# A two-layer graph attention and a neighbour sum: a tile's own-node product moved from the second to the third pass, and its seen edges added three steps ahead

## The chip, the core and the metric

The kernel runs on one core of a Trainium2 chip. The time is the device time of one execution, in microseconds (us). TensorE is called PE here (PEld its weight loads), VectorE DVE, ScalarE ACT, GpSimd POOL, and SyncE, which issues most transfers, SP.

## The reference, cut to what matters

There are N = 12500 nodes with 256 features and E = 200000 edges (`src`, `dst`, and a weight each).

```python
h = relu(layernorm(x))
e = h @ W_P_w + W_P_b + W_pos                 # 128 wide
for layer in range(2):                        # attention over the edges, 8 heads of 16
    q, k, v = (e[src] @ qT), (e[dst] @ kT), (e[dst] @ vT)
    att = exp(clip(sum_of_head(q * k), -10, 10))
    agg = segment_sum(att * v, src) / (segment_sum(att, src) + 1e-8)
    e = layernorm(agg + e) * ln_s + ln_b
x = x + e @ inv_w + inv_b                     # 256 wide
h = relu(layernorm(x))
agg = segment_sum(edge_weight * (h @ w_nbr)[src], dst)
out = x + agg + h @ w_own + bias
```

## The kernel before

Nodes lie in NT = 98 tiles of 128. A head (0 to about 650 us) sorts the edges, embeds the nodes and makes the plan of the edges, with a test (`bad`) that decides between a general and a short arm; these inputs take the short arm, `short_arm`. In it the order of the instructions on every engine is the order of the program text (a manual schedule); the waits between engines come from the tiles that they share.

**Two attention passes** (`short_attention`, layers 0 and 1). The edges of an attention layer are grouped by the tile of `src`. Edges whose other end is in the first SB = 3 tiles are "seen": SEEN = 3 columns of 128 edges a tile, whose keys and values are taken from `kvn` in SBUF by a one-hot product on PE. The others are "far": 1304 columns, STEP = 8 of them a step, 163 steps. For a far step POOL issues eight gathers (line 802) of k and v rows from DRAM into `kvg` (three buffers, issued two steps ahead); ACT spreads positions into one-hot tiles (L1186, L1190); PE takes the queries (`take_q`, L1205) from `q` by a tile number in a register; DVE makes the logits (L1215) and the weighted values; PE sums them by node into `ps` (`sums`, L1244 and L1246); DVE adds `ps` into `acc` (`adds`, L813).

The loop over the steps calls the far functions in a fixed order and, between them, the work that was put into named slots of that step:

```python
put(slots, (t0 - 5, "load", load), (t0 - 3, "act_seen", spread_hot), (t0 - 2, "pe_seen", take),
    (t0 - 2, "act_k", copy_k), (t0 - 2, "dve_seen", logits), (t0 - 2, "act_last", exps),
    (t0 - 1, "dve_seen_v", weighted), (t0 - 1, "pe_sums", sums), (t0, "dve_adds", add))
```

This is a tile's seen work (`seen`). A tile's far edges are complete at a step called `before` (at least one more than that of the tile ahead of it: 2, 4, 6, 7, 9, 11, 12, 14 ...). Before the change `seen` is given that step as `t0`, and so is what follows a tile's sums, `after`: in layer 0 `next_layer` (normalize, then the next q, k, v: `qkv`), in layer 1 `neighbour_rows`. That runs over some ten steps: normalize; `outwards` (L1012 to L1014: the product with `inv_w`, plus x by an identity product, plus the bias), kept in DRAM as `res_d`; a second normalization; `turn_c` (transpose), `relu` (ACT, into `ht`, L1046); `both` (L1051: products of `ht` with `w_nbr` and `w_own` side by side, 512 wide, and L1053, the bias onto the second half); `rows` (ACT: L1057 copies the first half for a store into the DRAM table `th`, L1059 copies the second half into `acc1`, two tensors of 128 columns that reuse `q` and `acc`); `store`.

**The third pass** (`short_neighbours`) groups the edges by the tile of `dst` in 196 steps of K2 = 8 columns. POOL gathers rows of `th` (L802) into `kvg`, two steps ahead; DVE makes weighted one-hot tiles one step ahead (`edge_hot`, L1343, two buffers); PE multiplies (`sums`, L1356 and L1358: two groups of four columns and one more product each); DVE adds into `acc1` (`adds`, L813). When a tile has all its columns, `result` adds `xt` (its rows of `res_d`, loaded by SP three steps ahead) to `acc1` in two additions (L1378) and stores the rows. Before a step's `sums` PE loads tile numbers of the next step into registers, from `near` (loaded by SP at L1312 for two steps). The order of a step is: transfers, gathers for t + 2, `edge_hot` for t + 1, `adds` of t − 1, results, registers for t + 1, `sums` of t.

Of the kernel before, what the change touches and what calls it, by code (L numbers as in the profile page):

```python
# [27 lines left out]
F32 = mybir.dt.float32  # L28
# [86 lines left out]
def gnn_kernel(ctx, tc, x, src, dst, edge_weight, wp_w, wp_b, w_pos, q1, k1, v1, ln1_s, ln1_b,  # L115
# [19 lines left out]
    part_neg = const.tile([P, SB], F32, name="part_neg")  # L135
    for b in range(SB):
        nc.vector.tensor_scalar(part_neg[:, b:b + 1], part_f, -1.0, float((1 - b) * P), op0=OP.mult, op1=OP.add)
    bad = const.tile([P, 9], F32, name="bad")
    nc.vector.memset(bad, 0.0)
    none = const.tile([1, P], BF16, name="none")  # L140
    nc.vector.memset(none, 0.0)
# [56 lines left out]
    emb_d = [dram.tile([NT * P, D], F32, name=f"emb{i}") for i in range(2)]  # L198
    last_d = dram.tile([NT * P, D], F32, name="last")
    res_d = dram.tile([NT * P, GD], F32, name="res")  # L200
    place_d = dram.tile([P, W], BF16, name="place_d")

    near_d = [dram.tile([1, CG * P // RC, RN], I32, name=f"near{i}") for i in range(2)]
# [13 lines left out]
    def rows_of(t):  # L217
        return min(P, N - t * P)
# [123 lines left out]
    def columns_out(pool, psum, a, b, c):  # L342
# [48 lines left out]
        by_step = lambda t: t[:, 0:FAR].rearrange("p (n k) -> p n k", k=STEP)  # L391
        firsts = t8[:, 0:FAR:STEP]
        fits = c[0:1, STEPS * (STEP + 2):STEPS * (STEP + 3)]
        nc.vector.tensor_tensor(fits, t8[:, STEP::STEP], firsts, op=OP.subtract)
        nc.vector.tensor_scalar(fits, fits, 1.0, None, op0=OP.is_gt)
        nc.vector.tensor_reduce(bad[0:1, 1:2], fits, AX.X, OP.max)
        nc.vector.tensor_scalar(fits, firsts, SLOPE, SLOPE + SLACK - 1.0, op0=OP.mult, op1=OP.add)
        nc.vector.tensor_tensor(fits, fits, step_row, op=OP.is_lt)
        nc.vector.tensor_reduce(fits[:, 0:1], fits, AX.X, OP.max)
        nc.vector.tensor_tensor(bad[0:1, 1:2], bad[0:1, 1:2], fits[:, 0:1], op=OP.add)  # L400
        nc.vector.tensor_scalar(t8, t8, float(NT - 1), None, op0=OP.min)
        nc.vector.tensor_copy(table[:, :, 0:STEP], by_step(t8))
        same = b[0:1, 0:FAR].rearrange("p (n k) -> p n k", k=STEP)
# [594 lines left out]
    def neighbour_rows(node, slots, weights, acc, acc1, t0, t):  # L998

        n = rows_of(t)  # L1000
        inv_sb, w2_sb = weights
        tiles, t1 = attended_later(node, slots, acc, t0, t, 1)
        t2 = even(t1 + 1)
        t3 = next_free(slots, "turn_c", t2 + 2)

        def load():
            xt = tiles["xt"] = node.tile([P, GD], F32, name="xt", bufs=2)
            nc.sync.dma_start(xt[:n], x[t * P:t * P + n, :])

        def outwards():  # L1010
            po = tiles["po"] = slots["psum"].tile([P, 4 * P], F32, name="out_e", tag="n1")
            nc.tensor.matmul(po[:n, 0:GD], tiles["et"][:, :n], inv_sb, start=True, stop=False)  # L1012
            nc.tensor.matmul(po[:n, 0:GD], ident[:n, :n], tiles["xt"][:n], start=False, stop=False)
            nc.tensor.matmul(po[:n, 0:GD], ones_b[:, :n], rows3[:, 0, :], start=False, stop=True)  # L1014

        def copy_all():
            y = tiles["all"] = node.tile([P, GD], F32, name="all", bufs=3)
            nc.scalar.copy(y[:n], tiles["po"][:n, 0:GD])

        def keep_all():  # L1020
            nc.sync.dma_start(res_d[t * P:t * P + n, :], tiles["all"][:n])

        def whole():
            tiles["mv"] = moments(node, tiles["all"][:n], n)

        def root():
            deviation(tiles["mv"], n, eps5)

        def normal():
            mv = tiles["mv"]  # L1030
            nc.vector.reciprocal(mv[:n, 1:2], mv[:n, 1:2])
            off = tiles["off"] = node.tile([P, 1], F32, name="off")
            nc.vector.tensor_scalar(off[:n], mv[:n, 0:1], mv[:n, 1:2], -1.0, op0=OP.mult, op1=OP.mult)

        def centred():
            c = tiles["c"] = node.tile([P, GD], F32, name="c", bufs=2)
            nc.scalar.activation(c[:n], tiles["all"][:n], AF.Identity, bias=tiles["off"][:n], scale=tiles["mv"][:n, 1:2])

        def turn_c():
            pt = tiles["pt2"] = slots["psum"].tile([P, 4, P], F32, name="turn_c", tag="n2")  # L1040
            for k in range(2):
                nc.tensor.transpose(pt[:, k, :n], tiles["c"][:n, k * P:(k + 1) * P], ident[:n, :n])

        def relu():
            ht = tiles["ht"] = node.tile([P, 2, P], F32, name="ht", bufs=1)
            nc.scalar.activation(ht[:, :, :n], tiles["pt2"][:, 0:2, :n], AF.Relu)  # L1046

        def both():
            pz = tiles["pz"] = slots["psum"].tile([P, 4 * P], F32, name="out_c", tag="n2")
            for k in range(2):  # L1050
                nc.tensor.matmul(pz[:n], tiles["ht"][:, k, :n], w2_sb[:, k].rearrange("p a b -> p (a b)"),  # L1051
                                 start=(k == 0), stop=False)
            nc.tensor.matmul(pz[:n, GD:], ones_b[:, :n], rows3[:, 1, :], start=False, stop=True)  # L1053

        def rows():
            h = tiles["h"] = node.tile([P, GD], F32, name="out_rows")
            nc.scalar.copy(h[:n], tiles["pz"][:n, 0:GD])  # L1057
            for h, to in enumerate(acc1):
                nc.scalar.copy(to[:n, t, :], tiles["pz"][:n, GD + h * D:GD + (h + 1) * D])  # L1059

        def store():
            nc.sync.dma_start(th[t * P:t * P + n, :], tiles["h"][:n])

        put(slots, (t1 - 1, "load", load), (t1, "pe_out", outwards), (t1 + 1, "act_out", copy_all),
            (t1 + 1, "store", keep_all), (t1 + 1, "dve_next", whole), (t2, "act_root", root), (t2 + 1, "dve_next", normal),
            (t2 + 1, "act_root", centred), (t3, "pe_turn", turn_c), (t3, "act_turn", relu),
            (t3, "pe_out", both), (t3 + 1, "act_out", rows), (t3 + 1, "store", store))

    def short_attention(wide, pool, psum, still, q, acc, layer, after, early=None):

# [88 lines left out]
                (t0 - 2, "act_k", copy_k), (t0 - 2, "dve_seen", logits), (t0 - 2, "act_last", exps),  # L1159
                (t0 - 1, "dve_seen_v", weighted), (t0 - 1, "pe_sums", sums), (t0, "dve_adds", add))  # L1160

        before = -1
        for t in range(NT):
            before = max(before + 1, (ends_by(t) - 1) // STEP + 1)
            seen(t, before)
            after(slots, before, t)

        def load(i):
# [134 lines left out]
            other_work("store")  # L1303
            t += 1

    def short_neighbours(wide, pool, psum, acc1, plan):
        steps = MAIN // K2
        of = {}

# [58 lines left out]
                f(i)  # L1368

        def load_own(t):  # L1370
            xt = of["xt", t] = pool.tile([P, GD], F32, name="xt", bufs=6)
            nc.sync.dma_start(xt[:rows_of(t)], res_d[t * P:t * P + rows_of(t), :])

        def result(t):
            n, xt = rows_of(t), of.pop(("xt", t))
            for h, to in enumerate(acc1):
                half = slice(h * D, (h + 1) * D)
                nc.vector.tensor_add(xt[:n, half], to[:n, t, :], xt[:n, half])  # L1378
            nc.sync.dma_start(out[t * P:t * P + n, :], xt[:n])


# [4 lines left out]
        for t in range(-4, steps + 1):  # L1386
            if t % 2 == 0:
                do(load, t // 2 + 2, steps // 2)
            for i in outs.get(t + 3 if t + 3 < steps else -1, ()):
                load_own(i)  # L1390
            if t == steps - 1:
                for i in outs[steps]:
                    load_own(i)
            if t == -4:
                for i in range(2):
                    do(gathers, i)
                next_tiles()
            if t >= 0:
                do(gathers, t + 2)
            do(edge_hot, t + 1)  # L1400
            do(adds, t - 1)
            if t < steps:
                for i in outs.get(t, ()):
                    result(i)
            do(registers, t + 1)
            do(sums, t)
        for i in outs[steps]:
            result(i)

    def short_arm(q, acc, acc1):  # L1410
        with tc.tile_pool(name="short", bufs=1) as wide, tc.tile_pool(name="short_p", bufs=1, space=PSUM) as psum, \
# [3 lines left out]
            nc.scalar.copy(still[:, 0:P], iota_f)  # L1415
            with tc.tile_pool(name="short_a", bufs=1) as pool, tc.tile_pool(name="short_n", bufs=2) as node:
                inv_sb = pool.tile([P, GD], F32, name="inv_sb")
                w2_sb = pool.tile([P, 2, 2, GD], F32, name="w2_sb")

                def load_weights():  # L1420
                    layer_rows(pool, True)
                    nc.sync.dma_start(inv_sb, inv_w)
                    for j, w in enumerate((w_nbr, w_own)):
                        nc.sync.dma_start(w2_sb[:, :, j, :], w.rearrange("(k p) n -> p k n", p=P))

                weights = (inv_sb, w2_sb)
                short_attention(wide, pool, psum, still, q, acc, 0,
                                lambda slots, t0, t: next_layer(node, slots, q, acc, t0, t), load_weights)
                short_attention(wide, pool, psum, still, q, acc, 1,
# [1 line left out]
            with tc.tile_pool(name="short_b", bufs=1) as pool:  # L1431
                weights = pool.tile([P, MAIN + MAIN // K], F32, name="plan2")
                nc.scalar.dma_start(weights[:, 0:MAIN], plan_d[2][:, 0:MAIN])
                plan = (idx_a, place_a[:, 0:MAIN + MAIN // K], weights)
                short_neighbours(wide, pool, psum, acc1, plan)


    def results(acc1):
# [66 lines left out]
    with tc.tile_pool(name="sort_a", bufs=1) as sp, tc.tile_pool(name="node_a", bufs=2) as node, \  # L1505
# [30 lines left out]
            embed(node, npsum, wp_sb, zb3, ones_b, q, (t,))  # L1536
        for _ in plan_as_they_come(cp, cpsum):
            pass
        pb = cpsum.tile([P, 9], F32, name="pb", tag="turned")
        nc.tensor.matmul(pb[0:1], ones[:, 0:1], bad, start=True, stop=True)  # L1540
        any_bad = cp.tile([1, 1], F32, name="any_bad")
        nc.vector.tensor_reduce(any_bad, pb[0:1], AX.X, OP.add)
# [37 lines left out]
```

## Time and profile before

| | |
|---|---|
| Median of 11 runs | 7351.35 us (7342.39 to 7369.84) |
| Profiled execution | 7346.42 us, span 7344.6 us |
| Mean granted TensorE clock | 0.802 |
| Busy, share of the span | PE 68%, PEld 56%, DVE 56%, ACT 37%, POOL 54% |
| First pass, first to last far sums | 692 to 2770 us |
| Second pass, first to last far sums | 2830 to 5042 us |
| Third pass, first to last gather | 5080 to 7332 us |

The times of a profile are those of the one profiled execution, on its own clock from the first instruction. In a group's line stand line, engine, operation and tile, the shape, the count, busy time and mean duration; in a list of waits the engine and line that waited, for what, the total, the times and the longest. "issue" is time in which an engine waited for nothing that the profile shows, "remote" a wait whose releaser the profile does not place. Ends of matmuls are modelled.

### The profile page before, as it was taken

How to read it: one execution, taken by the hardware profiler on the slowest of the kernel's cores; microseconds unless marked ns; L12 is line 12 of the kernel's file. 1: busy time of each engine (PE TensorE's matmuls, PEld its weight loads, DVE VectorE, ACT ScalarE, POOL GpSimd, SP SyncE). 2: the span in 40 equal slices, each digit the busy share in tenths (PEclk: the TensorE clock that was granted, in tenths of full speed). 3: DMA queues.
4: the chain of work that ended last, by engine and by line, in shares of the span. 5: the costliest groups of instructions: out<-in, count | busy, mean ns of one | idle time of the engine just before them, and what ended most of it. 6: DMA issues, size and time to landing. Idle time of an engine off the chain costs nothing. (4 is left out here: it accounts for less than half of the span.)

```text
span 7344.6 us, 91646 instructions
## 1 busy us (share of the span) xinstructions
PE 4969.0 (68%) x26262; PEld 4115.0 (56%) x26262; DVE 4096.3 (56%) x9525; ACT 2689.6 (37%) x4814; POOL 3980.4 (54%) x4189
## 2 busy tenths in 40 slices
PE   6773777777777776777777878777555555555555
PEld 3443666666666665666666666664444444444444
DVE  8776666666666665666666666664333333333334
ACT  3442555555555554555555555553000000000000
POOL 0002555555555554555555555554666666666666
PEclk7566888898888887988998888888777777777777
DMA  3112444444444443444444454443333333333333
GB/s 98 56 58 75 126 131 130 130 132 127 128 126 128 131 123 116 128 131 129 127 136 128 125 134 128 128 130 98 93 94 97 99 99 103 105 107 107 110 112 110
DMA packets 536717, 839.01 MB, mean 114 GB/s; under 512 B 105934, under 2 KB 360093, under 8 KB 536235
## 3 DMA queue, kind: packets, MB, share of 16 engines
q0 software_dynamic: 200448, 547.62, 25.7%
q1 hardware_dynamic: 334617, 284.29, 14.0%
q8 instruction: 245, 4.01, 0.2%
q14 instruction: 237, 1.94, 0.1%
q10 hardware_dynamic: 1170, 1.15, 0.1%
HBM read 752.73 MB, written 79.91 MB: 113 GB/s over the span
## 5 line engine op out<-in xcount | busy, mean ns | idle before, releaser
L802 POOL DMA_INDIRECT kvg<-tkv,idx_a x2608 | 2468.5, 947 | 2538.0 <-issue 1309.7
L802 POOL DMA_INDIRECT kvg<-th,idx_a x1568 | 1498.9, 956 | 812.8 <-issue 451.7
L1356 PE MATMUL ps<-kvg,hot 128*128 128x256 f32 x3136 | 1047.6, 482 | 1000.5 <-issue 890.1
L1356 PEld LDWEIGHTS ps<-kvg,hot 128*128 128x128 f32 x3136 | 757.4, 247 | 1225.1 <-issue 1053.2
L1343 DVE TENSOR_SCALAR hot<-iota_f,place_a,plan 128x128 f32<-128x128 f32 x1960 | 521.2, 360 | 1433.3 <-remote 1271.8
L1244 PE MATMUL ps<-kvg,hot 128*128 128x136 f32 x5216 | 838.2, 307 | 358.3 <-issue 339.3
L1215 DVE TENSOR_TENSOR kvg<-qe,kvg 128x512 f32<-128x512 f32 x652 | 431.5, 687 | 1106.4 <-remote 427.1
L1244 PEld LDWEIGHTS ps<-kvg,hot 128*128 128x128 f32 x5216 | 744.7, 210 | 448.1 <-issue 386.9
L1205 PE MATMUL qe<-q,hot_t 128*128 x5216 | 839.0, 312 | 131.0 <-issue 66.0
L1205 PEld LDWEIGHTS qe<-q,hot_t 128*128 128x128 f32 x5216 | 762.5, 224 | 174.4 <-issue 85.1
L1122 PE MATMUL qe<-kvn,hot_s 128*128 128x128 f32 x4720 | 704.2, 301 | 99.2 <-issue 97.6
L1122 PEld LDWEIGHTS qe<-kvn,hot_s 128*128 128x128 f32 x4720 | 659.6, 217 | 111.1 <-issue 110.1
L1186 ACT ACTIVATE far<-spread,part_neg 128x1280 bf16<-128x1280 bf16 x326 | 446.3, 1369 | 20.6 <-issue 9.8
L1190 ACT ACTIVATE hot_t<-far,ones 128x1280 f32<-128x1280 bf16 x326 | 444.9, 1365 | 0.5
L1229 DVE TENSOR_TENSOR hot<-still,place_a 128x1152 f32<-128x1152 f32 x326 | 439.4, 1348 | 0.0
L1153 PE MATMUL qe<-rows_s,hot_e 128*128 128x136 f32 x1176 | 233.7, 348 | 291.4 <-DVE rows_s L1145 214.3
L1234 DVE TENSOR_TENSOR kvg<-still,kvg 128x1024 f32<-128x1024 f32 x326 | 395.0, 1212 | 24.3 <-ACT kvg L1223 16.4
L1217 DVE TENSOR_REDUCE att<-kvg 128x64 f32<-128x1024 f32 x326 | 397.8, 1220 | 11.2
L1153 PEld LDWEIGHTS qe<-rows_s,hot_e 128*128 128x128 f32 x1176 | 194.8, 239 | 331.0 <-issue 239.0
L813 DVE TENSOR_TENSOR acc<-acc,ps 128x256 f32 (+1 forms) x718 | 304.9, 425 | 109.8 <-PE ps L1246 45.5
L1102 ACT ACTIVATE far<-seen,part_neg 128x256 bf16<-128x256 bf16 (+1 forms) x588 | 337.9, 639 | 0.8
L1358 PE MATMUL ps<-kvg,hot 128*128 x784 | 295.1, 463 | 32.8 <-issue 31.9
(253 smaller groups left out, 6492.2 us busy)
## 6 DMA issues: line engine op xcount, KB each, us to landing
spread<-place_d SPq DMA_DIRECT2D x326, 256.0 KB
kvg<-tkv,idx_a POOLq DMA_INDIRECT x2608
kvg<-th,idx_a POOLq DMA_INDIRECT x1568
xt<-in_x_dram SPq DMA_DIRECT2D x194, 128.0 KB
spread<-ext_d SPq DMA_DIRECT2D x326, 64.0 KB
seen<-place_d SPq DMA_DIRECT2D x196, 96.0 KB
seen<-other SPq DMA_DIRECT2D x196, 96.0 KB
emb<-e SPq DMA_DIRECT2D x194, 64.0 KB
```

The costliest lines, as they stand in the source:

```text
L802: nc.gpsimd.indirect_dma_start(out=dest, out_offset=None, in_=table, in_offset=bass.IndirectOffsetOnAxis(ap=idx, axis=0))
L1122: nc.tensor.matmul(to[:, k, :], hot_t[:, at, :], kvn[:, b, half], start=(i == 0), stop=(i == len(have) - 1))
L1153: nc.tensor.matmul(out_of, its["hot"][:, k, :], its["rows"][:, k, :], start=(k == 0), stop=(k == SEEN - 1))
L1186: nc.scalar.activation(far, of.pop(("spread", i)), AF.Abs, bias=part_neg[:, 1:2])
L1190: nc.scalar.activation(hot_t.rearrange("p k e -> p (k e)"), of.pop(("far", i)), AF.Relu, bias=ones[:, 0:1], scale=-1.0)
L1205: nc.tensor.matmul(qe[:, k, :], hot_t[:, h * K + k, :], q[:, bass.ds(tiles[h * K + k], 1), :], start=(k == 0), stop=False)
L1215: nc.vector.tensor_mul(kk, qe, kk)
L1217: nc.vector.tensor_reduce(att, kvg[:, :, 0:D].rearrange("p k (h d) -> p k h d", d=HD), AX.X, OP.add)
L1229: nc.vector.tensor_tensor(hot, iota_p[:, None, :].to_broadcast([P, STEP + 1, P]), place_a[:, c:c + STEP + 1, None].to_broadcast([P, STEP + ...
L1244: nc.tensor.matmul(ps[:, bass.ds(at, 1), :].rearrange("p a b -> p (a b)") if k else ps[:, 0, :], of["hot", i][:, k, :], of["kvg", i][:, k, ...
L1343: nc.vector.tensor_scalar(hot[:, k, :], iota_f, plan[1][:, c:c + 1], plan[2][:, c:c + 1], op0=OP.is_equal, op1=OP.mult)
L1356: nc.tensor.matmul(ps[:, bass.ds(at, 1), :].rearrange("p a b -> p (a b)") if k else ps[:, 0, :], hot[:, w * K + k, :], hg[:, k, :], start= ...
```

## The change

- The second pass makes only the product with `w_nbr` (`both` becomes two 256-wide products, with no bias). `ht` (relu of the normalized rows, transposed) is stored into a new DRAM tensor `ht_d`, 128 KB a tile; `ht` has two buffers in place of one. The two ACT copies into `acc1` go; two memsets on DVE clear the tile's part of `acc1` instead (`nothing`).
- The third pass loads `ht` and `xt` of a tile four steps ahead of its result (`xt` was loaded three ahead), and a new `own` on PE makes `ht` × `w_own` + `xt` (identity product) + bias in PSUM, behind the `sums` of the step ahead of the result. `result` adds that PSUM tile to `acc1`, again in two additions. `w_own` is loaded at the start of the third pass.
- In both attention passes a tile's seen work is put at `at`, at most three steps ahead of `before` (1, 2, 3, 4, 6, 8, 9, 11 ...); the work behind a tile's sums stays at `before`.
- In the test of the plan a partial result is put into a tenth column of `bad` in place of the second, and tile numbers are capped at NT ahead of it.

```diff
@@ neighbour_rows
         def relu():
-            ht = tiles["ht"] = node.tile([P, 2, P], F32, name="ht", bufs=1)
+            ht = tiles["ht"] = node.tile([P, 2, P], F32, name="ht", bufs=2)
             nc.scalar.activation(ht[:, :, :n], tiles["pt2"][:, 0:2, :n], AF.Relu)
         def both():
+            nc.sync.dma_start(ht_d[t][:, :, :n], tiles["ht"][:, :, :n])
             pz = tiles["pz"] = slots["psum"].tile([P, 4 * P], F32, name="out_c", tag="n2")
             for k in range(2):
-                nc.tensor.matmul(pz[:n], tiles["ht"][:, k, :n], w2_sb[:, k].rearrange("p a b -> p (a b)"),
-                                 start=(k == 0), stop=False)
-            nc.tensor.matmul(pz[:n, GD:], ones_b[:, :n], rows3[:, 1, :], start=False, stop=True)
+                nc.tensor.matmul(pz[:n, 0:GD], tiles["ht"][:, k, :n], w_sb[:, k], start=(k == 0), stop=(k == 1))
         def rows():
             h = tiles["h"] = node.tile([P, GD], F32, name="out_rows")
             nc.scalar.copy(h[:n], tiles["pz"][:n, 0:GD])
-            for h, to in enumerate(acc1):
-                nc.scalar.copy(to[:n, t, :], tiles["pz"][:n, GD + h * D:GD + (h + 1) * D])
+        def nothing():
+            for to in acc1:
+                nc.vector.memset(to[:, t, :], 0.0)
...
-            (t3, "pe_out", both), (t3 + 1, "act_out", rows), (t3 + 1, "store", store))
+            (t3, "pe_out", both), (t3 + 1, "act_out", rows), (t3 + 1, "dve_adds", nothing), (t3 + 1, "store", store))
@@ short_attention
-        before = -1
+        before, at = -1, 0
         for t in range(NT):
             before = max(before + 1, (ends_by(t) - 1) // STEP + 1)
-            seen(t, before)
+            at = max(at + 1, before - 3)
+            seen(t, at)
             after(slots, before, t)
@@ short_neighbours
         def load_own(t):
-            xt = of["xt", t] = pool.tile([P, GD], F32, name="xt", bufs=6)
-            nc.sync.dma_start(xt[:rows_of(t)], res_d[t * P:t * P + rows_of(t), :])
+            n = rows_of(t)
+            xt = of["xt", t] = pool.tile([P, GD], F32, name="xt", bufs=8)
+            nc.sync.dma_start(xt[:n], res_d[t * P:t * P + n, :])
+            ht = of["ht", t] = pool.tile([P, 2, P], F32, name="ht", bufs=7)
+            nc.sync.dma_start(ht[:, :, :n], ht_d[t][:, :, :n])
+        def own(t):
+            n, ht = rows_of(t), of.pop(("ht", t))
+            po = of["own", t] = psum.tile([P, 4 * P], F32, name="own", tag=f"n{1 + t % 2}")
+            for k in range(2):
+                nc.tensor.matmul(po[:n, 0:GD], ht[:, k, :n], own_sb[:, k], start=(k == 0), stop=False)
+            nc.tensor.matmul(po[:n, 0:GD], ident[:n, :n], of["xt", t][:n], start=False, stop=False)
+            nc.tensor.matmul(po[:n, 0:GD], ones_b[:, :n], rows3[:, 1, :], start=False, stop=True)
         def result(t):
-            n, xt = rows_of(t), of.pop(("xt", t))
+            n, xt, po = rows_of(t), of.pop(("xt", t)), of.pop(("own", t))
             for h, to in enumerate(acc1):
                 half = slice(h * D, (h + 1) * D)
-                nc.vector.tensor_add(xt[:n, half], to[:n, t, :], xt[:n, half])
+                nc.vector.tensor_add(xt[:n, half], po[:n, half], to[:n, t, :])
             nc.sync.dma_start(out[t * P:t * P + n, :], xt[:n])
...
-            for i in outs.get(t + 3 if t + 3 < steps else -1, ()):
+            for i in outs.get(t + 4, ()):
                 load_own(i)
-            if t == steps - 1:
-                for i in outs[steps]:
-                    load_own(i)
...
             do(registers, t + 1)
             do(sums, t)
+            for i in outs.get(t + 1, ())[:2]:
+                own(i)
-        for i in outs[steps]:
+        for k, i in enumerate(outs[steps]):
             result(i)
+            for j in outs[steps][k + 2:k + 3]:
+                own(j)
```

More of the change, by code (lines that the diff above doesn't have):

```diff
@@ L137, in gnn_kernel @@
         nc.vector.tensor_scalar(part_neg[:, b:b + 1], part_f, -1.0, float((1 - b) * P), op0=OP.mult, op1=OP.add)
-    bad = const.tile([P, 9], F32, name="bad")
+    bad = const.tile([P, 10], F32, name="bad")
     nc.vector.memset(bad, 0.0)
@@ L200, in gnn_kernel @@
     res_d = dram.tile([NT * P, GD], F32, name="res")
+    ht_d = dram.tile([NT, P, 2, P], F32, name="ht_d")
     place_d = dram.tile([P, W], BF16, name="place_d")
@@ L393, in columns_out @@
         fits = c[0:1, STEPS * (STEP + 2):STEPS * (STEP + 3)]
+        nc.vector.tensor_scalar(t8, t8, float(NT), None, op0=OP.min)
         nc.vector.tensor_tensor(fits, t8[:, STEP::STEP], firsts, op=OP.subtract)
         nc.vector.tensor_scalar(fits, fits, 1.0, None, op0=OP.is_gt)
-        nc.vector.tensor_reduce(bad[0:1, 1:2], fits, AX.X, OP.max)
+        nc.vector.tensor_reduce(bad[0:1, 9:10], fits, AX.X, OP.max)
         nc.vector.tensor_scalar(fits, firsts, SLOPE, SLOPE + SLACK - 1.0, op0=OP.mult, op1=OP.add)
@@ L399, in columns_out @@
         nc.vector.tensor_reduce(fits[:, 0:1], fits, AX.X, OP.max)
-        nc.vector.tensor_tensor(bad[0:1, 1:2], bad[0:1, 1:2], fits[:, 0:1], op=OP.add)
+        nc.vector.tensor_tensor(bad[0:1, 9:10], bad[0:1, 9:10], fits[:, 0:1], op=OP.add)
         nc.vector.tensor_scalar(t8, t8, float(NT - 1), None, op0=OP.min)
@@ L1000, in neighbour_rows @@
         n = rows_of(t)
-        inv_sb, w2_sb = weights
+        inv_sb, w_sb = weights
         tiles, t1 = attended_later(node, slots, acc, t0, t, 1)
@@ L1304, in short_attention, with short_neighbours @@
             t += 1
-    def short_neighbours(wide, pool, psum, acc1, plan):
+    def short_neighbours(wide, pool, psum, acc1, plan, own_sb):
         steps = MAIN // K2
@@ L1417, in short_arm @@
                 inv_sb = pool.tile([P, GD], F32, name="inv_sb")
-                w2_sb = pool.tile([P, 2, 2, GD], F32, name="w2_sb")
+                w_sb = pool.tile([P, 2, GD], F32, name="w_sb")
                 def load_weights():
@@ L1422, in load_weights @@
                     nc.sync.dma_start(inv_sb, inv_w)
-                    for j, w in enumerate((w_nbr, w_own)):
-                        nc.sync.dma_start(w2_sb[:, :, j, :], w.rearrange("(k p) n -> p k n", p=P))
-                weights = (inv_sb, w2_sb)
+                    nc.sync.dma_start(w_sb, w_nbr.rearrange("(k p) n -> p k n", p=P))
+                weights = (inv_sb, w_sb)
                 short_attention(wide, pool, psum, still, q, acc, 0,
@@ L1434, in short_arm @@
                 plan = (idx_a, place_a[:, 0:MAIN + MAIN // K], weights)
-                short_neighbours(wide, pool, psum, acc1, plan)
+                own_sb = pool.tile([P, 2, GD], F32, name="own_sb")
+                nc.scalar.dma_start(own_sb, w_own.rearrange("(k p) n -> p k n", p=P))
+                short_neighbours(wide, pool, psum, acc1, plan, own_sb)
     def results(acc1):
@@ L1538, in gnn_kernel @@
             pass
-        pb = cpsum.tile([P, 9], F32, name="pb", tag="turned")
+        pb = cpsum.tile([P, 10], F32, name="pb", tag="turned")
         nc.tensor.matmul(pb[0:1], ones[:, 0:1], bad, start=True, stop=True)
```

## The prediction

> **What bounds it now.** I read the busy slices first, for the stages; then busy time by stretch, one row to a pass.
>
> ```profile
> span 7344.6 us, 91646 instructions
> ...
> PE   6773777777777776777777878777555555555555
> ...
> POOL 0002555555555554555555555554666666666666
> PEclk7566888898888887988998888888777777777777
> ...
> 700.00:2770.00 2070.00, 1499.29 (x9883) 1385.38 (x9883) 1326.94 (x2660) 1113.57 (x1752) 1207.03 (x1275) 0.86 0.45 128
> 2830.00:5040.00 2210.00, 1752.87 (x10831) 1484.13 (x10831) 1381.79 (x2845) 1266.05 (x2215) 1210.24 (x1280) 0.89 0.45 128
> ...
> 6100.00:6600.00 500.00, 270.94 (x885) 210.88 (x884) 180.79 (x650) 0.00 (x0) 332.94 (x349) 0.74 0.36 105
> ```
>
> The columns are length, then busy PE, PEld, DVE, ACT, POOL, then granted clock, DMA share, GB/s. Two attention passes of 163 steps (12.83 and 13.65 us between far sums) are led by PE: 72% and 79% busy, where DVE has 64 and 63%, ACT 54 and 57%, POOL 58 and 55%. In the third pass (196 steps of 11.5 us) ACT does nothing and PE is 54% busy. POOL's eight gathers need 8 × (0.95 + 0.30) = 10.0 us of a step, the floor.
>
> The waits view of 5100 to 7330 us says what stands still there, and the timeline shows one such stall:
>
> ```profile
> DVE hot L1343 <- remote: 1271.8, 113, 26.5
> ...
> PE ps L1356 <- issue: 889.7, 241, 12.5
> ...
> POOL kvg L802 <- remote: 285.0, 93, 4.7
> ...
> 6207.66 0.41 PEld L1358 LDWEIGHTS ps<-kvg,hot 128*128 128x128 f32 x2
> 6207.88 0.59 PE L1358 MATMUL ps<-kvg,hot 128*128 x2
> ...
> 6213.51 0.94 POOL L802 DMA_INDIRECT kvg<-th,idx_a  x1 [0.30 <-issue]
> 6217.56 2.65 DVE L1343 TENSOR_SCALAR hot<-iota_f,place_a,plan 128x128 f32<-128x128 f32 x10 [14.69 <-remote]
> 6217.79 0.94 POOL L802 DMA_INDIRECT kvg<-th,idx_a  x1 [3.34 <-remote]
> ...
> 6220.98 3.75 PE L1356 MATMUL ps<-kvg,hot 128*128 128x256 f32 x8 [12.50 <-issue]
> ```
>
> PE stands idle 12.5 us; DVE and POOL go on together at 6217.6, though the sums whose buffers they wait for end in the records by 6204.2 (step 96, counting 20 matmul records a step). Either PE's completion is seen late, or a landing 2 to 3 us after the last gather (6213.51) lets them go. So about one POOL group in two waits 2 to 5 us, and the step is 11.5, not 10.0 us.
>
> The rows of what moves:
>
> ```profile
> L1051 PE MATMUL out_c<-w_sb,ht x392: 589/592/1123, 2950.8 to 5073.1; 128*128 128x512 f32 x194, 128*84 128x512 f32 x2
> ...
> L1053 PE MATMUL out_c<-rows,ones_b x98: 264/278/391, 2953.2 to 5073.6; 3*128 3x256 bf16 x97, 3*84 3x256 bf16 x1
> L1059 ACT COPY acc<-out_c x98: 274/285/287, 2956.1 to 5074.4; 128x128 f32<-128x128 f32 x97, 84x128 f32<-84x128 f32 x1
> L941 DVE MEMSET acc<- x98: 172/172/172, 710.3 to 2775.9; 128x136 f32 x98
> L1378 DVE TENSOR_TENSOR xt<-q,xt x98: 275/284/290, 5438.0 to 7341.0; 128x128 f32<-128x128 f32 x97, 84x128 f32<-84x128 f32 x1
> L1356 PE MATMUL ps<-kvg,hot x3136: 376/379/796, 5083.5 to 7338.0; 128*128 128x256 f32 x196
> ```
>
> **The change, part by part.** The sum is made on the profiled execution: 7346.4 us, its span and 1.8 us around it, 5 us under the median of 7351.35.
>
> *Product halved in pass 2.* The matmul records overlap, so I take the time from the end of the matmul before `both` to the start of the one behind it: median 1.86, mean 2.59 us over 92 tiles. The like for the half left over is `outwards` (four 256-wide f32 records and a bias): median 1.20, mean 1.81, about 0.2 less without the bias. Saved: 0.86 to 1.2 us a tile; I take 1.2, since the half-clock tiles count in the time: 98 × 1.2 = 118 us of PE. How much of it is time? Pass 2 is 140 us longer than pass 1 with 254 us more PE: 0.55. Steps with `both` are 2.8 us longer than those without, for 2.59 us of PE: 1.07, but other work of the tile stands in them too. I take 0.7, nearer the first: **−83 us** (−46 by 0.86 × 98 × 0.55, −126 by 118 × 1.07). With less PE work the clock could fall: pass 1 has 0.86 at 72% busy, pass 2 0.89 at 79%. PE goes to (1753 − 118) / (2210 − 83) = 77%, so −0.01, 1% of 1753 us, 18 × 0.7 = +12 at worst, inside these ends. The Trainium skill ("TensorE: Matmul & The Clock Gate", Part 1) says that the clock is full or half only and falls after an idle window of some 3.4 us; by it nothing is lost where a burst is merely shorter, and the sum keeps 0.
>
> *Copies and memsets.* ACT loses 98 × (0.27 + 0.285) = 54 us; ACT is 57% busy and has nothing queued that ends a step: 0. DVE gains 98 × 2 × 0.17 = 34 us ahead of `weighted` and `edge_hot`, which the far sums need; `take_q` waits too, as it reads q by register. DVE waits over a third of the step: **+5** (0 to +34).
>
> *DMA.* SP issues the new ht store behind ACT's relu of the same step, with the row stores and the next step's loads queued behind it. Spread loads are three steps ahead, so 13 us of cover; uncovered, ACT's spread and PE's `take_q` come late by the relu's wait, a few us a tile. 25 MB on 839 at a DMA share of 0.45: 0 (to +20).
>
> *Seen edges three steps ahead.* Same instructions on other steps. Collisions of a tile's `take` with the previous tiles' products change (pass 1, with q/k/v: 3 of 6 tiles to 4; pass 2, with `both`: 4 of 6 to 3, with `outwards`: 3 to 4). Weighing mean step lengths of before by the new counts of each mixture gives +0.19 and +0.25 us a step (+72 us over both passes); by coarser groups of pass 2 only +0.03 (+5). Some groups hold two steps, so I go near the coarse end: **+10** (−20 to +72). In the tails of the passes, where nothing else hides it, the last tile's seen work goes: **−5** (0 to −10).
>
> *Own product in pass 3.* A tile gets three f32 256-wide products (two records each, 0.2145 us apart at full clock by L1356's rows) and a bias: 1.4 us, at half clock 2.8; 98 tiles 137 to 274 us of PE. It stands behind sums(t), ahead of sums(t+1), so in PE's burst or in its 5 us a step of idle time. Steps with and without a result tile are alike now (11.50 against 11.42), but results use DVE and SP, not PE. The result's adds only change operand: 0.28 us, 0.295 for the nearest add from PSUM. Loads are four steps ahead and the product one step ahead of the result, so 34 us of cover against the 20.6 us that SP sits at one wait for `near`. If that fails, PE stops at `own` with sums(t+1) behind it, and POOL two groups on. Bounds: all of it on the path, +274; none, 0; below nothing, POOL's floor, 196 × 1.5 = −294, if PE's completions become visible sooner because more PE work follows them. I take **0**: PE idles 46% and POOL's gathers pace the step. The skill speaks against this ("Perfetto Trace Analysis", Per-engine timelines): a TensorE end is estimated, the semaphore comes only after PSUM's acknowledgement. If the late releases here are PE truly still working, its idle time is not there, and the sum would be +64 to +201.
>
> Sum: −83 + 5 + 10 − 5 + 0 = **−73**: 7273 by the profiled execution, 7278 beside the median.
>
> **Rivals.**
>
> 1. *Own products not hidden (slower).* For: `hot` and POOL wait for what only PE releases. Against: 46% of PE idle, and POOL at 10.0 of 11.5 us. Price +137 to +274, in all 7415 to 7552; half hidden, about 7350 to 7420. It decides from 73 / 98 = 0.75 us more a tile.
> 2. *Seen work collides worse.* +72 in place of +10, conversion 0.55 (−65): +7 − 5 + 5 = about +7, 7358; with −46 for the product 7377. For: in pass 2 it is the longest steps that hold `take` beside a product. It decides from +0.25 us a step in pass 1, where nothing else changes.
> 3. *Third pass nears its floor.* For: POOL waits at `kvg` in half its groups and goes on late after the sums. Against: nothing shows what ends that wait. A third of 294: −98 more, about 7180; at 0.5 us a step and above it outweighs the rest.
> 4. *Nothing arrives.* Steps of pass 2 set by the chain through DVE and ACT, whose idle shares (37 and 43%) speak against it: 7340 to 7365.
>
> **Chances.** Forecast 0.46 (own range 7225 to 7320); rival 1 0.26; rival 2 0.12; rival 3 0.12; rival 4 0.04. About 0.2%, or 15 us, can be told from no change. The forecast and rival 3 are faster: 0.58. A tenth of rival 1, a third of rival 2 and rival 4 make no difference: 0.11. The rest is slower: 0.31. The range runs from a third pass a little past rival 3 (7150) to rival 1 nearly unhidden (7435); left out are the dear half of rival 1 (0.13) and the far end of rival 3 (0.04).
>
> **What would show it.** Right: pass 2 (2829.6 to 5041.5 now) 60 to 100 us shorter with PE near 77%; pass 1 within 15 us; third pass within 20 us of 2252, with `own` in or behind the sums' burst. Wrong: steps of the third pass with `own` longer by 0.75 us or more, POOL's remote wait over 285 us; or pass 1, where only the seen edges move, 30 us longer.

## The result, and the profile after

The changed kernel took 7398.9 us (median of 8 runs, 7392.0 to 7415.0), the kernel before 7352.4 (31 runs): 46 us more, a ratio of 1.0062 (95% interval 1.0051 to 1.0073). The forecast was 73 us less. The profiled execution took 7405.5 us. Of the signs set ahead two came true: pass 1 stayed within 15 us and the third pass within 20 us of 2252. Pass 2, which was to be 60 to 100 us shorter, became longer.

The page's slices after:

```profile
span 7403.7 us, 93154 instructions
...
PE   6774777777777776777777777776555555566666
...
PEclk7566888888888887888888888888777777777777
```

PE's last slices stand at 6 where they stood at 5: the own products grow denser towards the end of the third pass. The busy time by stretch, for the second pass (first to last far sums) and for the gathers of the third, first before and then after (columns as in the prediction: length, PE, PEld, DVE, ACT, POOL, clock, DMA share, GB/s):

```profile
2829.60:5041.50 2211.90, 1754.63 (x10846) 1485.69 (x10845) 1381.79 (x2845) 1267.84 (x2221) 1210.24 (x1280) 0.89 0.45 128
5079.80:7330.80 2251.00, 1226.38 (x3901) 941.45 (x3902) 817.39 (x2926) 0.00 (x0) 1498.01 (x1568) 0.72 0.36 103
...
2841.70:5096.40 2254.70, 1700.86 (x10725) 1534.40 (x10723) 1388.52 (x3027) 1227.05 (x2027) 1213.75 (x1280) 0.86 0.46 131
5124.70:7379.40 2254.70, 1358.11 (x4540) 1017.04 (x4541) 813.33 (x2908) 0.00 (x0) 1488.36 (x1567) 0.74 0.38 108
```

Stage by stage in the two traces (a pass runs from the start of the last far sum of its first step to that of its last step, the third pass from gather to gather):

| us | before | after | more |
|---|---|---|---|
| Start to first far sums | 692.3 | 687.8 | −4.5 |
| First pass | 2078.0 | 2092.1 | +14.1 |
| Between the passes | 59.3 | 61.7 | +2.4 |
| Second pass | 2211.9 | 2254.7 | +42.8 |
| To the first gather of `th` | 38.3 | 28.3 | −10.0 |
| Third pass, gathers | 2250.9 | 2254.8 | +3.9 |
| From the last gather to the end | 13.9 | 24.2 | +10.3 |

PE's busy time in the second pass fell from 1754.6 to 1700.9 us, and the pass became longer all the same: PE stood idle for 457 us of it before and for 554 after. Which waits grew is seen in POOL's list. The same stretch, waits of POOL alone, before and then after:

```profile
POOL kvg L802 <- issue: 330.5, 1082, 0.6
POOL kvg L802 <- PE ps L1246: 301.1, 63, 13.8
POOL kvg L802 <- PE turn_c L1042: 185.1, 45, 7.4
POOL kvg L802 <- PE turn_e L960: 80.4, 18, 6.6
POOL kvg L802 <- PE qe L1122: 57.8, 23, 3.3
POOL kvg L802 <- remote: 26.9, 11, 2.7
```

```profile
POOL kvg L804 <- PE ps L1251: 398.8, 76, 16.0
POOL kvg L804 <- issue: 321.0, 1050, 0.6
POOL kvg L804 <- PE turn_c L1044: 174.3, 34, 7.7
POOL kvg L804 <- remote: 67.4, 28, 2.6
POOL kvg L804 <- PE qe L1125: 41.3, 17, 2.7
POOL kvg L804 <- PE turn_e L962: 14.0, 5, 3.4
```

POOL's own work is 1304 gathers either way, so its waits have to grow by about as much as the pass. The lines other than "issue" sum to 651 us before and 696 after: +45, beside the pass's +43. Such a sum comes out for any engine whose work stays the same (DVE's waits other than "issue" go from 745 to 795 us), so it does not show by itself what sets the pace. What it does show is that the waits put down to PE stay at 624 and 628 us in all, with more for the far sums (`ps`) and less for `turn_e`, and that those without a releaser go from 27 to 67.

The third pass hid the own products: 2254.8 against 2250.9 us, with 132 us more PE in it. Its waits after:

```profile
DVE hot L1348 <- remote: 1117.7, 92, 25.8
...
POOL kvg L804 <- remote: 235.7, 75, 4.8
```

### The profile page after: what moved, and what is told of

Same layout as the page of the kernel before. It is cut to its first block, busy times and chain, and to the rows that moved or that the text cites. A ratio compares the mean times of both kernels' runs of the same rounds, so it can differ in the third digit from the quotient of the medians.

```text
span 7403.7 us, 93154 instructions
## 1 busy us (share of the span) xinstructions
PE 5059.6 (68%) x26850; PEld 4256.2 (57%) x26850; DVE 4106.8 (55%) x9722; ACT 2649.0 (36%) x4614; POOL 3976.4 (54%) x4189
## 5 line engine op out<-in xcount | busy, mean ns | idle before, releaser
L1361 PE MATMUL ps<-kvg,hot 128*128 128x256 f32 x3136 | 993.9, 462 | 680.4 <-issue 531.7
L1249 PE MATMUL ps<-kvg,hot 128*128 128x136 f32 x5216 | 896.4, 322 | 366.4 <-issue 346.5
L1210 PE MATMUL qe<-q,hot_t 128*128 x5216 | 856.9, 316 | 167.1 <-issue 89.4
L1125 PE MATMUL qe<-kvn,hot_s 128*128 128x128 f32 x4720 | 686.6, 297 | 115.8 <-issue 88.2
L1111 ACT ACTIVATE hot_s<-far,ones 128x1280 f32<-128x1280 bf16 x196 | 267.2, 1363 | 238.5 <-remote 99.4
```

Source lines behind the costliest of these rows:

```text
L1125: nc.tensor.matmul(to[:, k, :], hot_t[:, at, :], kvn[:, b, half], start=(i == 0), stop=(i == len(have) - 1))
L1210: nc.tensor.matmul(qe[:, k, :], hot_t[:, h * K + k, :], q[:, bass.ds(tiles[h * K + k], 1), :], start=(k == 0), stop=False)
L1249: nc.tensor.matmul(ps[:, bass.ds(at, 1), :].rearrange("p a b -> p (a b)") if k else ps[:, 0, :], of["hot", i][:, k, :], of["kvg", i][:, k, ...
L1361: nc.tensor.matmul(ps[:, bass.ds(at, 1), :].rearrange("p a b -> p (a b)") if k else ps[:, 0, :], hot[:, w * K + k, :], hg[:, k, :], start= ...
```

## The experiments

Theory A: the seen edges' new steps are the loss, the own move by itself a gain. Theory B: the own move does not pay. The runs came from five chips. On four of them the kernel before took 6050 to 6053 us, on the fifth 7225, in the first comparison 7352; what differs is taken up at the end. The time of a run is compared with that of the kernel before on its own chip only. Stages come from one profiled execution each and are also compared across the four chips of 6050 us: there pass 2 took 1698.8 and 1700.0 us in two profiles of the kernel before, and 1620.4, 1620.6 and 1626.5 in three of `e1_own_only`.

**One part alone (chip of 6052 us).** `e1_own_only`:

```diff
-            seen(t, at)
+            seen(t, before)
```

> The changed kernel with the seen work put back to `before`: only the own product is moved. Theory A (the seen edges' new steps collide with the tile's other PE work; the own move by itself is a gain): pass 2 60 to 100 us shorter than before, pass 1 unchanged, third pass within 10 us; time about 7270 to 7310. Theory B (the own move does not pay: what it adds on SP and DVE holds pass 2 up, the seen edges matter little): pass 2 0 to 40 us longer, time 7350 to 7400.

Measured: 5970.5 us, ratio 0.9868 (0.9853 to 0.9883), that is −82 us. `e2_seen_only` is the kernel before with

```diff
-            seen(t, before)
+            at = max(at + 1, before - 3)
+            seen(t, at)
```

> The kernel before with the seen work three steps ahead and nothing else. Theory A: pass 1 +14 us as in the changed kernel, pass 2 +100 to +140; time 7440 to 7490. Theory B: pass 1 +14, pass 2 +0 to +20; time 7350 to 7380.

Measured: 6107.9 us, ratio 1.0091 (1.0077 to 1.0105), +56 us: as to sign theory A, in size half of what it expected. The next run has five in place of three in the changed kernel:

```diff
-            at = max(at + 1, before - 3)
+            at = max(at + 1, before - 5)
```

> The changed kernel with the seen work five steps ahead in place of three. Three tiles end in five steps, so five ahead puts a tile's seen work on the same kinds of steps as in the kernel before, though earlier. Theory A as a matter of which work meets on a step: as e1_own_only within 15 us, so 7270 to 7310. Theory A as a matter of being early (buffers, waits): no better than the changed kernel, 7390 to 7430. Theory B: as the changed kernel, 7380 to 7410.

Measured: 5990.4 us, ratio 0.9896 (0.9881 to 0.9911), 20 us above e1_own_only and not within the 15. Its passes are e1's within 2 us; in the profiles, which lie 30 us apart, the first far sums come 17 us later and the time between the passes is 13 us longer, see below. So on this chip it is not the earliness that makes the passes longer. `e4_no_own` leaves the own product out altogether:

```diff
-                nc.tensor.matmul(pz[:n], tiles["ht"][:, k, :n], w2_sb[:, k].rearrange("p a b -> p (a b)"), ...
+                nc.tensor.matmul(pz[:n, 0:GD], tiles["ht"][:, k, :n], w2_sb[:, k, 0, :], start=(k == 0), stop=(k == 1))
```

> The kernel before with the own product left out (its 256 columns, the bias, the two copies), with the memsets put in; rows kept in DRAM and the third pass as before. The output lacks that product. It prices the halved product alone. Theory A: pass 2 60 to 100 us shorter, third pass the same, time 7260 to 7295, within 15 us of e1_own_only. Theory B: either the halving gives nothing (7340 to 7360), or it gives its 60 to 100 us and e1_own_only lies that much above this one, which puts the cost on the store of ht and the loads.

Measured: 5968.8 us, ratio 0.9863 (0.9848 to 0.9879): the same as e1_own_only within 2 us. So the store of `ht`, the loads and the products in the third pass cost nothing that can be told on this chip; theory B falls there.

**The changed kernel on such a chip.**

> The changed kernel once more, as the four runs before this one stood on a chip where the kernel before takes 6052 us and not 7351. On a chip of the 6052 kind: the parts add (own move -82, seen edges +56): 5.98 to 6.04 thousand us, 10 to 50 us faster than before there, with pass 2 some 55 us longer than in e1_own_only. If the parts do not add (the slower result of the first comparison holds on every chip): 6080 to 6110. On a chip of the 7351 kind: 7390 to 7410 again.

Measured: 6017.4 us, ratio 0.9939 (0.9925 to 0.9953): here the changed kernel is 34 us faster. The parts add within 8 us (−82 + 56 = −26).

> e1_own_only once more. On a chip of the 6052 kind: 5970 within 10 us. On a chip of the 7351 kind, theory A (seen edges are the loss there too): pass 2 60 to 100 us shorter than before, 7270 to 7310; theory B (there the own move does not pay): 7350 to 7400.

Measured: 5964.3 us, ratio 0.9852 (0.9837 to 0.9867), on the same chip as c_after.

**Stages, start, and slack.**

> The kernel before, for a profile on the chip of the experiments. On a chip of the 6052 kind: pass 1 within 5 us of e4_no_own (1619), third pass 1966, and pass 2 some 1670 to 1680 (from the medians: e1_own_only lies 82 us under before, 50 of which should be in pass 2). On a chip of the 7351 kind: 2078, 2212 and 2251 us as before.

Measured: 6046.2 us. Pass 2 took 1698.8 us, not 1670 to 1680. The stages of all these runs, from their traces:

| us | first far sums at | pass 1 | between | pass 2 | third pass | last gather to end |
|---|---|---|---|---|---|---|
| d_before | 664.6 | 1620.5 | 41.7 | 1698.8 | 1967.7 | 12.6 |
| e1_own_only | 670.5 | 1617.6 | 40.9 | 1620.4 | 1966.1 | 17.1 |
| e4_no_own | 666.9 | 1619.4 | 39.6 | 1627.0 | 1966.8 | 12.7 |
| e2_seen_only | 683.9 | 1617.0 | 55.5 | 1727.6 | 1967.8 | 12.5 |
| c_after | 689.3 | 1616.4 | 55.0 | 1642.6 | 1966.6 | 16.6 |
| e3_five_ahead | 687.9 | 1619.2 | 54.3 | 1620.4 | 1965.1 | 16.3 |
| g2_start_at_two | 673.6 | 1622.6 | 45.7 | 1653.6 | 1965.0 | 17.3 |

The own move takes 78 us from pass 2 (73 between k_before and k_own, on one chip). The seen edges three ahead add 29 us to pass 2 with the whole product and 22 with the half, and 13 to 19 us at each start of a pass. Five ahead adds nothing to pass 2, and the same at the starts. The 162 steps of a pass between its first and last far sums are 1620 us at eight gathers of 1.25 us: pass 1 is at POOL's floor in every row, pass 2 in e1 and e3, not in d_before and c_after. POOL's waits in pass 2 say the same. d_before:

```profile
POOL kvg L802 <- issue: 327.7, 1074, 0.6
POOL kvg L802 <- PE ps L1246: 40.9, 31, 3.0
POOL kvg L802 <- PE turn_e L960: 34.0, 15, 3.9
POOL kvg L802 <- PE qe L1122: 17.1, 33, 3.0
```

e1_own_only:

```profile
POOL kvg L804 <- issue: 340.6, 1118, 0.3
POOL kvg L804 <- PE qe L1125: 7.0, 23, 0.3
```

c_after:

```profile
POOL kvg L804 <- issue: 334.5, 1097, 0.6
POOL kvg L804 <- PE ps L1251: 31.3, 13, 9.2
POOL kvg L804 <- PE qe L1125: 8.4, 21, 1.7
POOL kvg L804 <- PE turn_e L962: 7.8, 10, 1.5
```

e2_seen_only:

```profile
...
POOL kvg L802 <- PE ps L1247: 76.5, 25, 9.6
POOL kvg L802 <- PE turn_e L960: 41.9, 15, 4.1
POOL kvg L802 <- PE qe L1122: 13.8, 27, 2.6
```

A wait of 0.3 us is the usual gap between gathers; what is above that is a late buffer. Summed over pass 2 it is 2 us in e1, 5 in e4, 15 in e3, 37 in c_after, 71 in d_before and 118 in e2, nearly in the order of the lengths of pass 2. `ps` is the far sums. That PE comes to them late where steps with much seen and node work stand together is a reading of the steps, taken up below; no run isolates it.

`g2_start_at_two` keeps the first tile's seen work where it was:

```diff
-        before, at = -1, 0
+        before, at = -1, 1
```

> The changed kernel with the first tile's seen work at step 2 as in the kernel before (`at` starts from 1), all later ones three steps ahead. If the 14 us that c_after starts pass 1 later and the 14 us more between the passes come from the first tiles' seen work ahead of the first far steps: 25 to 30 us under c_after, about 5990, pass 2 still 1640. If they come from elsewhere: 6010 to 6025. If pass 2 loses by being early and not by what meets: no change either.

Measured: 6006.8 us, ratio 0.9931 (0.9915 to 0.9948), 11 us under c_after (on another chip of 6050 us) where 25 to 30 were expected. The starts give back 16 and 9 us, and the two passes took 17 more; that part was not foreseen, and its cause is open.

`g3_own_thrice` makes each own product three times:

```diff
-            for k in range(2):
-                nc.tensor.matmul(po[:n, 0:GD], ht[:, k, :n], own_sb[:, k], start=(k == 0), stop=False)
...
+            for again in range(3):
+                for k in range(2):
+                    nc.tensor.matmul(po[:n, 0:GD], ht[:, k, :n], own_sb[:, k], start=(k == 0), stop=False)
...
```

> e1_own_only with the own product of a tile made three times into the same sum (so three times that product and x in the output). It asks how much idle time of PE is left in the third pass. With 26% of PE idle there and two products more at 1.4 to 2.8 us on half of the steps: the third pass stays at 1966 to 1985 us, its end 5 us later. If the product was just hidden and the next one shows (rival 1's point of decision is near): 2100 to 2240 us. On a chip of the 7351 kind the same question against 2251 us.

Measured: 5979.1 us in one run; the third pass 1965.8 us as with one product, the end 26.5 instead of 17.1. Its stretch of the gathers:

```profile
3984.90:5950.80 1965.90, 1615.42 (x5900) 1060.82 (x5901) 828.06 (x2932) 0.00 (x0) 1488.53 (x1568) 0.95 0.42 124
```

PE is 82% busy there, and POOL keeps its pace: rival 1 is far from its point of decision on such a chip.

**On a chip nearer to the first.** Two runs came from the chip where the kernel before took 7224.9 us. There is one time of each of the three, so some 20 us of doubt: the 31 runs of the kernel before in the first comparison lie between 7330 and 7375 us.

> e1_own_only once more, to see it under the conditions of the first comparison, if they come back (kernel before at 7351 us). There, if the product saved in the second pass is swallowed by waits for PE's late completions (the step with `take` beside two products took 18.3 us with the whole product and with the half): pass 2 within 25 us of 2212, time 7330 to 7360. If it is saved as in the runs at 6050: pass 2 60 to 90 us shorter, time 7260 to 7300. At 6050 again: 5970 within 10 us.

> e2_seen_only once more, for the same reason. Under the conditions of the first comparison, if the seen work's new steps are the loss there: pass 1 +14 us, pass 2 +40 to +70, time 7400 to 7440. If the own move is the loss: 7350 to 7375. At 6050 again: 6108 within 10 us.

Measured: h1_own_only 7198.2 us, −27; h2_seen_only 7290.6 us, +66. Together +39, where the first comparison has +46. So there the seen edges are the loss, and the own move looks like a gain a third as large as on the other chips, though −27 is little more than the doubt. The kernel before was not profiled on that chip, and from h1 to h2 both parts differ: pass 1, where only the seen edges change, is 12 us longer, the start 16, pass 2 67 us (2137.8 to 2205.2, the halved product in it), the third pass 7 us shorter. POOL's waits in pass 2, h1_own_only and then h2_seen_only:

```profile
...
POOL kvg L804 <- PE ps L1251: 241.1, 59, 12.8
POOL kvg L804 <- PE turn_c L1044: 180.4, 49, 5.9
POOL kvg L804 <- PE turn_e L962: 74.4, 19, 5.6
POOL kvg L804 <- PE qe L1125: 57.2, 24, 3.2
POOL kvg L804 <- remote: 18.5, 8, 2.5
```

```profile
POOL kvg L802 <- PE ps L1247: 336.8, 72, 16.0
...
POOL kvg L802 <- PE turn_c L1042: 186.8, 45, 8.6
POOL kvg L802 <- PE qe L1122: 54.8, 21, 6.7
POOL kvg L802 <- PE turn_e L960: 47.5, 13, 5.3
POOL kvg L802 <- remote: 20.7, 9, 2.4
```

572 against 647 us: +75, beside the pass's +67, and here nearly all of it in the waits put down to PE.

**Three more runs, on a chip of 6050 us.**

> The kernel before, for its stages on the chip of the next two runs. On a chip of the slow kind (7200 to 7350): pass 2 some 30 us longer than in k_own, the other stages within 10 us of it.

> e1_own_only in rounds. On a chip of the slow kind, if the single look of h1_own_only holds: 15 to 40 us under before, with pass 2 some 30 us shorter where it is 78 shorter on the fast kind. If the own move is the whole loss of the changed kernel there: 20 us or more above before. On the fast kind 82 to 87 us under before again.

> e3_five_ahead in rounds. On a chip of the slow kind, if the loss of the seen edges is a matter of which work meets: pass 1 and pass 2 within 10 us of k_own, the whole 0 to 25 us above it. If it is a matter of being early: 40 us or more above k_own, near the changed kernel. On the fast kind 20 us above k_own again.

Measured: k_before 6046.2 us, k_own 5964.1 (ratio 0.9851, 0.9838 to 0.9864), k_five 5990.5 (0.9897, 0.9882 to 0.9912), as in e1 and e3; pass 2 was 1700.0, 1626.5 and 1618.0 us. Whether five ahead is harmless on a chip of 7200 us or more was not seen.

The version that beats both kernels is e1_own_only, by 1.3 to 1.5% on the chips of 6050 us and by 0.4% in its one run at 7225.

## Why the prediction was wrong

Both parts of the change were mis-sized, by 50 to 60 us each, as far as the chip of 7225 us stands for the first comparison: the seen edges measured +66, where the sum has +10 and −5, and the own move −27, where it has −83, +5 and 0. Together the measured two give +39, beside the +46 of the first comparison. The time still lies within the stated range, but its upper end was there for own products left on the path, which did not happen: that part is luck.

**The step that failed: the seen edges, +10.** They cost 66 us on the chip of 7225 us (one run) and 56 at 6050; in the first comparison itself pass 1, where nothing else changes, became 14 us longer. The prediction had two estimates, +72 by the fine mixtures of work on a step and +5 by coarse ones of pass 2, and went to the coarse end because some groups hold two steps. The fine end was the nearer one: of the 66 us some 16 lie at the start (h1 to h2), which no grouping held, 12 in pass 1, 3 between the passes and, by difference, about 35 in pass 2. The coarse groups throw together steps with and without `outwards`, and that is what the change exchanges: of 150 steps of pass 2, 45 had `take` beside `outwards` before and 59 after. Steps with both take 16.7 (without `both`) to 18.3 us in the trace after, steps with `outwards` and no `take` 10.7 to 12.5 before. For the chip of 7225 us an estimate can be made from the two traces: the mean length in h1 of each kind of step (with or without `take`, `outwards` and `both`), weighed by how often it occurs in h2, gives +30 us over pass 2 (one of the kinds rests on a single step of h1). At 6050 us this is not how the seen edges cost: there a step with `take` and `outwards` but not `both` takes 9.1 us. It is the steps with `take` alone that grow, from 7.7 us in d_before to 9.1 in e2_seen_only; 14 of these 31 now stand directly behind a step with all three and take 10.4. Rival 2 had the mechanism at +72 and 0.12; its 7358 to 7377 us are nearest, and 22 us or more short.

**The product, −83.** At 6050 the halved product took 78 us from pass 2 with 102 us less PE (1520.8 to 1418.7), a rate of 0.77 for 0.7. On the chip of 7225 us the whole own move brought about 27, in one run. The rate was taken from whole passes. It should have been read in the steps that hold the product. One such step (`take`, `both` and `outwards`, and no sums of a seen tile; such steps take 18.3 us in the mean before and after alike, with PE busy for 14.3 and for 13.2 us of them), from far sums to far sums, before:

```profile
3571.80:3590.20 18.40, 14.24 (x83) 11.53 (x82) 9.71 (x20) 10.33 (x21) 9.86 (x11) 0.91 0.48 139
```

after:

```profile
3598.70:3616.60 17.90, 13.22 (x83) 11.37 (x82) 10.90 (x21) 7.87 (x14) 8.54 (x9) 0.91 0.40 122
```

d_before, the same kind of step:

```profile
2877.30:2888.70 11.40, 11.40 (x83) 9.54 (x82) 9.55 (x22) 8.76 (x20) 8.51 (x9) 1.00 0.60 186
```

e1_own_only:

```profile
2860.30:2870.50 10.20, 10.20 (x83) 9.59 (x81) 9.76 (x22) 8.04 (x15) 7.64 (x9) 1.00 0.72 215
```

At 6050 PE is busy for the whole step, and 1.2 us less work is 1.2 us less time. In the first comparison PE stood idle for 4.2 of 18.4 us and afterwards for 4.7 of 17.9: half of the 1.0 us saved became waiting, and over all such steps, with the seen edges moved too, all of it did. The trace before showed these 4 idle microseconds. The price of 1.2 us a tile itself was right (11.39 to 10.15 us, the mean of such steps at 6050). Beside the waiting there is a second loss, the clock, below.

**The third pass, 0.** Right within a few us (+3.9, −1.6 from d_before to e1_own_only, +7 from h2 to h1). Rival 1 did not occur: at 6050 three products instead of one were hidden too. Rival 3 did not either.

**The end and the tails.** The tail of pass 2 gave 10 us where 5 was taken, but not for the reason given, that the last tile's seen work goes. At 6050 us that stretch is 38.6 us in d_before, 40.8 in e2_seen_only, where only the seen work moves, and 29.7, 35.2 and 30.6 in the three runs of e1_own_only: it is shorter with the own move, and that the −5 had the right sign was luck. The sum had no term for the end. The last tiles' own products stand behind the last sums, in the timeline after:

```profile
...
7396.97 1.13 PE L1387 MATMUL own<-own_sb,ht 128*128 128x256 f32 x4
...
7398.67 1.09 PE L1387 MATMUL own<-own_sb,ht 128*84 128x256 f32 x4
...
7400.68 0.28 DVE L1395 TENSOR_TENSOR xt<-own,acc 84x128 f32<-84x128 f32 x1
```

Three products of some 1.7 us each stand there, and the end is 4 to 5 us longer at 6050, 6 from h2 to h1 and 10 in the first comparison. The start of a pass, +13 to 19 us at 6050, was not in the sum either: the first tiles' seen work now stands ahead of the first far steps. In the first comparison it did not show.

**Copies, memsets, DMA: 5.** No run prices them alone: e4_no_own has the memsets and lacks the copies, as e1_own_only does. The store of `ht`, the loads and the own products are within the 2 us between the two at 6050; the +5 itself stays open.

**The clock.** The granted clock of pass 2 fell from 0.89 to 0.86 with the work taken out, more than the 0.01 that was allowed, and from 0.97 to 0.96 at 6050. The sum kept 0 for this, and that was too little. The clock of the traces takes only the values 1.0 and 0.5. At 1.0 PE was busy for 1323 us of pass 2 before and 1153 after, at 0.5 for 432 and 548. Counting time at 0.5 as half, 112 us of work went, as many as between d_before and e1_own_only; but the lower clock gave 58 us back, so that busy time fell by 54 only, and at 6050 by 102. The idle window by which the prediction kept the 0 does not fit the records: of 89 falls of the clock in pass 2 before, 3 have a gap of 3.4 us or more between PE's records in the 10 us ahead of them. Whether the clock fell because PE waited more, or the other way round, no run shows. What the Trainium skill ("Perfetto Trace Analysis", Per-engine timelines) says of a TensorE end, that it is estimated and the semaphore comes after, was weighed as a case against the change. At 6050 it makes no difference: `hot` starts within 0.1 us of the modelled end of the sums that it waits for, at the median. In the first comparison it starts 10.8 us after it before the change, and still PE had room for the own products.

## What to carry to other kernels

Read what a saved instruction is worth in the very steps that hold it: where the engine is busy for the whole step it is worth its duration, where it stands idle for a quarter of it the saving may only widen a wait. Where a fine and a coarse grouping disagree on what moving work costs, ask which of the two still separates the pairs of work that the move exchanges, and look at what stands in the step ahead, too. And do not take a sum of waits for a cause: the waits of an engine whose work stays the same, here POOL's, must change as the pass does. Such a list says which waits grew; what sets the pace is shown by runs that change one part, as here e3_five_ahead and g3_own_thrice do, or by a pass that reaches the floor of an engine.

## What the runs showed of the hardware

Chips differ by a fifth for the same program: 6050 us on four, 7225 on one, 7352 in the first comparison, whose chip is not known. Durations of single DVE, ACT and POOL instructions are alike (a gather 0.95 us on both). What differs in the records is PE's granted clock and when PE's completions are seen. The waits of DVE for PE's sums in the third pass, d_before:

```profile
L1343 DVE TENSOR_SCALAR hot<-iota_f,place_a,plan x1960: 327/340/570, 4066.6 to 6019.0; 128x128 f32<-128x128 f32 x196
...
  PE ps L1358: 1138.9, 194
```

There every wait has its releaser; in the first comparison 113 of these waits have none that the profile places. In d_before the semaphore of PE moves about once to each group of sums (5041.24, 5046.73, 5051.08, 5056.51 us) and stands for 7.3 us at most once the third pass runs. In the trace before of the first comparison it stands for over 10 us 107 times, for up to 34, and then moves in a bunch (6180.18, then 6194.36, 6194.47, 6194.58; 6202.01, then 6217.53, 6217.64), and PE's granted clock in the third pass is 0.72 and not 0.89. The chip of 7225 us shows the same (97 times over 10 us in h2_seen_only). In such a pause PE's records spread out, and DVE and ACT go on together at its end, as in the step after that was shown above:

```profile
3612.99 0.28 PE L1249 MATMUL ps<-kvg,hot 128*128 128x136 f32 x1 [1.83 <-issue]
...
3613.71 2.85 PE L1249 MATMUL ps<-kvg,hot 128*128 128x136 f32 x11 [0.44 <-issue]
3613.81 1.29 DVE L1220 TENSOR_TENSOR kvg<-qe,kvg 128x512 f32<-128x512 f32 x2 [3.61 <-remote]
3613.98 0.37 ACT L1058 COPY out_rows<-out_c 128x256 f32<-128x256 f32 x1 [3.98 <-remote]
```

What causes the pauses is open. The same change is 0.6% slower in the first comparison, with them, and 0.6% faster on a chip without them; that the pauses decide the sign is likely, but no run shows it apart from the lower clock, which goes with them.
